# Zeroing the exponentials of later keys on GpSimd in two causal attentions

## The chip, the cores and the metric

The kernel runs on one core of a Trainium2 chip. The time is the device time of one execution in microseconds (us); for the kernel before, three runs are shown and their median is taken. One further execution was taken by the hardware profiler, and all durations of single instructions come from it. The engines are named as in the profile: PE is TensorE (its matmuls; PEld its weight loads), DVE is VectorE, ACT is ScalarE, POOL is GpSimd, and SP issues DMAs.

## The reference

The reference is a decoder of four layers, each with self-attention, cross-attention and a feed-forward part, on an input of 8 sequences of 256 tokens and 256 features. After each part comes `x = layernorm(x + part(x))`. Two of the self-attentions, those of layers 1 and 2, are causal with 16 heads of 16 features:

```python
attn = jnp.einsum('bqhd,bkhd->bhqk', q, k) * scale
causal = jnp.tril(jnp.ones((T, T), dtype=bool))
attn = jnp.where(causal, attn, -jnp.inf)
attn = jax.nn.softmax(attn, axis=-1)
out = jnp.einsum('bhqk,bkhd->bqhd', attn, v).reshape(B, T, C)
return out @ Wo + bo
```

(This is layer 2. Layer 1 has rotary positions on q and k and no bias.) Everything else of the reference is untouched by the change.

## The kernel before

The parts of the network run one after the other; the weights of the next part are loaded while one runs. The tokens are kept as `X` (tokens on partitions) and transposed as `xT` (features on partitions).

The two causal attentions are `l1_attn` (line 760) and `l2_attn` (line 730). Both hand a projection to `attention16` (line 593), which goes through the 8 sequences, called batches here. Queries and keys of two batches are projected at once (`pair`, line 600): batches 0 and 1 ahead of everything, batches 2 and 3 after batch 0, and so on, so batches 1, 3 and 5 have a projection right in front of them, and batches 2, 4 and 6 have none.

The softmax of a batch is made in two passes over the scores. First, `largest16` (line 451) computes scores with queries on partitions, and DVE takes the largest of each row. There are three steps: `short(0)` for the first 128 queries, and `long(0)` and `long(1)` for the last 128 queries and all 256 keys, each for half of the heads. `lower16` (line 491) transposes the negated maxima on PE and puts them into spare rows of the queries. Second, `exps16` (line 503) computes the scores again with keys on partitions; the maximum is now subtracted by the matmul itself, and ACT takes the exponentials straight from PSUM to SBUF. Here, too, there are three steps: `first(0)` and `first(1)` for the first 128 keys and all 256 queries (tile `e0`, one for each half of the heads), and `second` for the last 128 keys and the last 128 queries of all heads (tile `e1`). In both passes later keys are kept out by a mask: a matmul of the identity with a 128x128 tile that holds -1e30 above or below the diagonal is put into the PSUM bank first, and the scores are added to it (`four_banks`, line 432, which works on four banks of PSUM, four heads' groups at a time). `sums16` (line 555) multiplies the exponentials with the values; `divided16` (line 535) turns and divides the result, its last multiplication (line 553, tile `aT`) on POOL.

The steps of different batches are interleaved by hand in `attention16`: while batch b is exponentiated, the maxima of batch b+1 are taken (`ahead`), and the output projection of batch b-1 with its layer norm runs after the first of the three exponential steps (`before[0]`), its transposition at the end (`before[1]`). In the layer norm, DVE computes the statistics, POOL the reciprocal root (`rs_v` line 141 and `rs_y` line 143), and DVE then writes the normalised `X` in two instructions (line 187). The instructions of one engine run in the order in which they stand in its queue. The scores, the sums and the projections share 8 PSUM banks in turn (`bank`, line 408), so a set of four scores can start only once what stood in its banks has been read.

What the kernel prints below are the functions that the change touches and their callers.

Of the kernel before, what the change touches and what calls it, by code (L numbers as in the profile page):

```python
# [12 lines left out]
BF16 = mybir.dt.bfloat16  # L13
# [3 lines left out]
ALU = mybir.AluOpType  # L17
# [3 lines left out]
P = 128  # L21
# [21 lines left out]
class Net:  # L43
    def __init__(self, ctx: ExitStack, tc: tile.TileContext, ins, out):
        self.tc, self.nc, self.ins, self.out = tc, tc.nc, ins, out
        nc = self.nc
        self.const = ctx.enter_context(tc.tile_pool(name="const", bufs=1))
        self.wpool = ctx.enter_context(tc.tile_pool(name="weights", bufs=1))
        self.tmp = ctx.enter_context(tc.tile_pool(name="tmp", bufs=3))
        self.ps_t = ctx.enter_context(tc.tile_pool(name="ps_t", bufs=2, space=PSUM))  # L50

        self.ident = self.const.tile([P, P], F32, name="ident")
        make_identity(nc, self.ident)
        self.ones = self.const.tile([1, P], F32, name="ones")
        nc.gpsimd.memset(self.ones, 1.0)

        self.X = self.const.tile([P, NT, D], F32, name="X")
        self.xT = self.const.tile([P, 2, NTOK], F32, name="xT")
        self.xT4 = self.xT.rearrange("p c (t n) -> p c t n", n=P)
        for b in range(B):  # L60
            nc.sync.dma_start(
                self.X[:, 2 * b : 2 * b + 2, :],
                ins["x"][b].rearrange("(t p) d -> p t d", p=P),
            )
        self.cols = self.const.tile([P, ins["cols"].shape[1]], F32, name="cols")
        nc.scalar.dma_start(self.cols, ins["cols"])
        self.consts = self.const.tile([P, ins["consts"].shape[1]], F32, name="consts")
        nc.scalar.dma_start(self.consts, ins["consts"])
        self.earlier = self.const.tile([P, P], BF16, name="earlier")
        nc.vector.tensor_copy(self.earlier, self.cst("earlier"))  # L70
        self.causal = self.const.tile([P, P], BF16, name="causal")
        nc.vector.tensor_scalar(self.causal, self.cst("later"), -1e30, None, ALU.mult)

        self.later_k = self.const.tile([P, P], BF16, name="later_k")
        nc.vector.tensor_scalar(self.later_k, self.cst("sooner"), -1e30, None, ALU.mult)
        self.other = self.const.tile([P, P], BF16, name="other")
        nc.vector.tensor_scalar(self.other, self.cst("other"), -1e30, None, ALU.mult)
        self.ident_bf = self.const.tile([P, P], BF16, name="ident_bf")
        nc.vector.tensor_copy(self.ident_bf, self.ident)
        self.ones_bf = self.const.tile([P, P], BF16, name="ones_bf")  # L80
        nc.gpsimd.memset(self.ones_bf, 1.0)
        self.ctxT = self.const.tile([P, 2, NCTX], F32, name="ctxT")
        nc.scalar.dma_start(self.ctxT, ins["ctxT"].rearrange("p (c n) -> p c n", c=2))
        self.gate1 = self.const.tile([P, 2, 32], F32, name="gate1")
        nc.scalar.dma_start(self.gate1, ins["l1f_gate"].rearrange("p (c n) -> p c n", c=2))
        self.avg = self.const.tile([P, 2, B], F32, name="avg")
        self.w_scale = self.const.tile([P, len(L2X)], F32, name="w_scale")
        self.half = self.const.tile([P, 2], F32, name="half")
        nc.gpsimd.memset(self.half, -0.5)
        self.power = False  # L90
        dram = ctx.enter_context(tc.tile_pool(name="dram", bufs=1, space=bass.MemoryType.DRAM))

        self.xd1 = dram.tile([NTOK + 1, D], F32, name="xd1")
        self.one = self.const.tile([P, 1], F32, name="one")
        nc.gpsimd.memset(self.one, 1.0)
        self.wset = 0
# [406 lines left out]
    def exps16(self, qv, kv, sizes, causal, work):  # L503

        nc = self.nc
        rows = [slice(32 * r, 32 * r + 32) for r in range(4)]
        later = self.later_k.unsqueeze(1)
        n0 = sizes[0]
        e0 = [work.tile([P, 4, 2, 2 * P], F32, name="e0") for m in range(2)]
        e1 = work.tile([P, 4, 4, P], F32, name="e1", bufs=1) if causal else None  # L510

        def first(m):
            self.four_banks(
                [n0, 2, 2 * P],
                (lambda sc: sc[:, :, :P], later.to_broadcast([P, 2, P])) if causal else None,
                lambda r: [(u, kv[rows[r], u, m, :n0], qv[rows[r], u, m, :]) for u in range(2)],
                lambda r, sc: nc.scalar.activation(e0[m][:n0, r], sc, AF.Exp),  # L517
            )

        def second():  # L520
            self.four_banks(
                [P, 4, P],
                (lambda sc: sc, later.to_broadcast([P, 4, P])),
                lambda r: [
                    (2 * m + u, kv[rows[r], u, m, P:], qv[rows[r], u, m, P:]) for m in range(2) for u in range(2)
                ],
                lambda r, sc: nc.scalar.activation(e1[:, r], sc, AF.Exp),
            )

        def e(m, r, u, kb):  # L530
            return e1[:, r, 2 * m + u, :] if kb else e0[m][:n0, r, u, :]

        return [lambda: first(0), lambda: first(1)] + ([second] if causal else []), e

    def divided16(self, out, av, work, parts=1):

# [1362 lines left out]
def layouts(inp):  # L1899
# [74 lines left out]
    for n in "qkvo":  # L1974
# [6 lines left out]
    p = np.arange(P, dtype=np.float32)  # L1981
# [14 lines left out]
            ("cos", rope_cos),  # L1996
            ("sin", rope_sin),
            ("other", (p[:, None] % 16 != p[None] % 16).astype(np.float32)),
            ("sooner", (p[:, None] > p[None]).astype(np.float32)),
            ("earlier", (p[:, None] < p[None]).astype(np.float32)),  # L2000
        ],
        LAYOUT.consts,
# [45 lines left out]
```

## Time and profile before

| what | value |
|---|---|
| median of 3 runs | 2792.79 us (2783.5 to 2794.55) |
| the profiled execution | 2775.67 us |
| its span, first to last instruction | 2773.9 us |
| mean granted PE clock over the span | 0.873 |
| PE, DVE, ACT, POOL busy, share of the span | 78%, 61%, 35%, 32% |
| l1_attn, about 563 to 761 us: PE, POOL busy | 183.0 and 35.5 of 198 us |
| l2_attn, about 1290 to 1446 us: PE, POOL busy | 140.1 and 24.2 of 156 us |
| mask matmuls of `later_k` (line 440) | 192, of 256 or 512 columns |

Busy time adds up what an engine spends inside instructions; a wait for another engine is not in it. The profiler models the ends of matmuls, so how long a row of matmuls takes is better read from the start of one group to the start of the next. In the timeline, a line gives the start, the length, the engine, the source line and operation, the tile written and the tiles read, and in brackets how long the engine stood idle before it and what released it. Several instructions of one kind that follow one another are merged into one line (x4).

### The profile page before, as it was taken

Reading aid. Unit: us, or ns where it says so; the run is one execution under the profiler, and the core shown is the slowest. Engines: PE = TensorE matmul, PEld = TensorE weight load, DVE = VectorE, ACT = ScalarE, POOL = GpSimd, SP = SyncE. Lnnn points to the kernel's source line nnn. Section 1 sums busy time; section 2 is a strip of 40 time slices with the busy share of each in tenths; the row PEclk is TensorE's granted clock in tenths of the full one; section 3 lists DMA queues with packets and bytes.
Section 4 is the critical chain, followed back from the end, with each engine's and each line's share of the span. In section 5 each row is a group of like instructions: output and inputs, shape, how many; then the busy total and the mean of one; then the engine's idle time right before and its main releaser. Section 6 shows DMA issues by size and latency. Waiting matters only on the chain.

```text
span 2773.9 us, 40937 instructions
## 1 busy us (share of the span) xinstructions
PE 2171.2 (78%) x14331; PEld 1571.3 (57%) x14331; DVE 1681.6 (61%) x5714; ACT 957.4 (35%) x2197; POOL 891.8 (32%) x949
## 2 busy tenths in 40 slices
PE   8978688699988788438975767887878868777975
PEld 5554588555565467415544345666756656555654
DVE  4654300266667575356767876758668666654876
ACT  2322133234333442104432333343534435433431
POOL 1020121221111124451110136666566565660000
PEclk9988699899998779759997878889989888887987
DMA  2001243200010137420010011111111111120000
GB/s 81 2 1 42 105 149 108 69 7 1 1 62 16 36 106 220 141 80 1 1 42 16 1 65 46 45 43 47 38 41 47 40 43 43 52 73 3 1 20 12
DMA packets 84173, 135.04 MB, mean 49 GB/s; under 512 B 33445, under 2 KB 53045, under 8 KB 82048
## 3 DMA queue, kind: packets, MB, share of 16 engines
q0 software_dynamic: 52288, 79.27, 9.7%
q1 hardware_dynamic: 28924, 49.45, 5.3%
q10 hardware_dynamic: 2756, 3.72, 0.4%
q8 instruction: 114, 1.87, 0.3%
q14 instruction: 91, 0.75, 0.1%
HBM read 242.90 MB, written 17.70 MB: 94 GB/s over the span
## 4 chain that ended last, share of the span: by engine, by line
PE 25%; DVE 16%; issue 6%; ACT 3%; another core or an unknown queue 2%; POOL 2%; DMA 0%; ACTq 0%; POOLq 0%; DVEq 0%
PE po L1401 5%; PE pp L132 4%; PE s L132 4%; PE po L132 3%; DVE junk L1349 2%; DVE low L478 1%; PE ph L132 1%; PE s L1547 1%; PE sc L132 1%; PE s L1525 1%; POOL rows L893 1%; PE po L1382 1%; PE sc L445 1%; DVE X L187 1%
## 5 line engine op out<-in xcount | busy, mean ns | idle before, releaser
L893 POOL DMA_INDIRECT rows<-in_l2f_table_dram,index x512 | 530.5, 1036 | 348.8 <-issue 110.7
L1401 PE MATMUL po<-rows,diag 128*128 128x256 f32 x768 | 231.2, 437 | 90.7 <-ACT diag L1400 54.4
L1349 DVE SCALAR_TENSOR_TENSOR junk<-rows,X 128x256 f32<-128x256 f32 x512 | 214.9, 420 | 53.6 <-DMA rows<-in_l2f_table_dram,index 28.4
L1401 PEld LDWEIGHTS po<-rows,diag 128*128 128x128 f32 x768 | 153.0, 213 | 142.8 <-ACT diag L1400 67.2
L132 PE MATMUL pp<-xT,w 128*128 128x256 f32 (+1 forms) x672 | 196.9, 435 | 35.1 <-issue 20.4
L132 PE MATMUL ph<-xeT,we 128*128 128x128 f32 x1248 | 183.7, 291 | 20.9 <-DMA we<-in_l0f_experts_dram,wrow 16.5
L132 PEld LDWEIGHTS ph<-xeT,we 128*128 128x128 f32 x1248 | 170.1, 201 | 41.7 <-DMA we<-in_l0f_experts_dram,wrow 17.9
L553 POOL TENSOR_TENSOR aT<-sides,inv 128x256 f32<-128x256 f32 x64 | 46.8, 731 | 441.6 <-DVE sides L551 275.3
L132 PEld LDWEIGHTS pp<-xT,w 128*128 128x128 f32 x672 | 141.6, 218 | 69.2 <-issue 29.7
L1400 ACT ACTIVATE diag<-ident,dots 128x128 f32<-128x128 f32 x384 | 134.1, 394 | 129.9 <-PE po L1401 58.8
L173 PE MATMUL pt<-ident,X 128*128 128x128 f32 x352 | 76.3, 330 | 117.6 <-DVE X L187 68.9
L174 ACT COPY xT<-pt 128x512 f32<-128x512 f32 x88 | 51.6, 587 | 328.1 <-PE pt L173 229.7
L893 POOL DMA_INDIRECT xe<-xd,take x87 | 85.2, 979 | 208.0 <-PE pt L908 81.6
L141 POOL TENSOR_SCALAR rs_v<-ln_mv 128x2 f32<-128x2 f32 x48 | 12.5, 260 | 389.8 <-DVE ln_mv L164 362.1
L173 PEld LDWEIGHTS pt<-ident,X 128*128 128x128 f32 x352 | 49.4, 163 | 152.7 <-issue 73.0
L132 PE MATMUL py<-we,hT 128*128 128x256 f32 x496 | 129.8, 386 | 0.9 <-DVE hT L1037 0.9
L1014 DVE TENSOR_TENSOR y<-py,we 128x256 f32<-128x256 f32 x23 | 9.8, 425 | 199.0 <-PE py L132 199.0
L517 ACT ACTIVATE e<-sc 128x512 f32<-128x512 f32 (+1 forms) x155 | 82.0, 602 | 107.2 <-PE sc L445 93.5
L1008 ACT ACTIVATE hT<-ph,we 128x128 f32<-128x128 f32 x184 | 65.5, 367 | 121.0 <-PE ph L132 91.3
L187 DVE TENSOR_SCALAR X<-z,ln_mv,rs_y 128x256 f32<-128x256 f32 x192 | 73.3, 424 | 54.3 <-POOL rs_y L143 52.4
L445 PE MATMUL sc<-kv,qv 32*128 32x128 f32 (+2 forms) x1448 | 99.8, 315 | 2.5 <-DVE sides L551 1.0
L445 PE MATMUL sc<-qv,kv 32*128 32x128 f32 (+2 forms) x1396 | 99.1, 347 | 0.0
(492 smaller groups left out, 5205.2 us busy)
## 6 DMA issues: line engine op xcount, KB each, us to landing
we<-in_l1f_experts_dram SPq DMA_DIRECT2D x32, 384.0 KB
yd<-y SPq DMA_DIRECT2D x32, 256.0 KB
rows<-in_l2f_table_dram,index POOLq DMA_INDIRECT x512
w<-in_l2x_w_dram SPq DMA_DIRECT2D x1, 4096.0 KB
yd<-y SPq DMA_DIRECT2D x23, 128.0 KB
X<-in_x_dram SPq DMA_DIRECT2D x8, 256.0 KB
xd<-X ACTq DMA_DIRECT2D x8, 256.0 KB
xd<-X SPq DMA_DIRECT2D x8, 256.0 KB
```

The source lines that it names most:

```text
L132: self.nc.tensor.matmul(out, lhsT=lhsT, rhs=rhs, start=n == 0, stop=n == last and bias is None)
L173: nc.tensor.transpose(pt[:, c, j, :], self.X[:, i0 + j * step, c * P : (c + 1) * P], self.ident)
L174: nc.scalar.copy(self.xT4[:, :, i0 : i0 + step + 1 : step, :], pt)
L187: nc.vector.tensor_scalar(self.X[:, i, :], z[:, j, :], mv[:, j, 0:1], r[:, j : j + 1], ALU.subtract, ALU.mult)
L445: nc.tensor.matmul(sc[: shape[0], part], lhsT=lhsT, rhs=rhs, start=mask is None, stop=True, skip_group_check=True)
L517: lambda r, sc: nc.scalar.activation(e0[m][:n0, r], sc, AF.Exp),
L553: nc.gpsimd.tensor_tensor(out, split(both), split(inv), ALU.mult)
L893: self.nc.gpsimd.indirect_dma_start(out=out, out_offset=None, in_=table, in_offset=bass.IndirectOffsetOnAxis(ap=index, axis=0), **({} if r ...
L1008: nc.scalar.activation(hT[:, g + f, :], ph[:, f, :], AF.Gelu, bias=b1[:, g + f : g + f + 1])
L1349: nc.vector.scalar_tensor_tensor(junk, row, 1.0, self.X[:, i, :], ALU.mult, ALU.mult, accum_out=out)
L1400: nc.scalar.activation(diag, self.ident, AF.Copy, scale=dots[:, k : k + 1])
L1401: nc.tensor.matmul(po, lhsT=diag, rhs=rows[:, k, D:], start=False, stop=g + k == H * K - 2)
```

## The change

The mask `later_k` goes out: the tile, the constant it was made from, and the mask matmuls in the three exponential steps. The scores of later keys are therefore exponentiated as they are. After each step, one affine selection on POOL goes over the exponentials of that step in place and writes 0 where the key (partition) comes after the query (last index). The selection of `first` covers the first 128 queries of each head, [128, 4, 2, 128] elements, with gaps between the rows of 128; that of `second` covers all of `e1`, [128, 4, 4, 128]. The maxima keep their own mask (`causal`). Last, the step `second` is put ahead of `first(0)` and `first(1)`.

```diff
-        self.later_k = self.const.tile([P, P], BF16, name="later_k")
-        nc.vector.tensor_scalar(self.later_k, self.cst("sooner"), -1e30, None, ALU.mult)
...
-        later = self.later_k.unsqueeze(1)
         n0 = sizes[0]
+
+        def no_later(e):
+
+            nc.gpsimd.affine_select(
+                out=e, in_=e, compare_op=ALU.is_ge, fill=0.0, base=0,
+                pattern=[[0, n] for n in e.shape[1:-1]] + [[1, P]], channel_multiplier=-1,
+            )
         e0 = [work.tile([P, 4, 2, 2 * P], F32, name="e0") for m in range(2)]
         e1 = work.tile([P, 4, 4, P], F32, name="e1", bufs=1) if causal else None
 
         def first(m):
             self.four_banks(
                 [n0, 2, 2 * P],
-                (lambda sc: sc[:, :, :P], later.to_broadcast([P, 2, P])) if causal else None,
+                None,
                 lambda r: [(u, kv[rows[r], u, m, :n0], qv[rows[r], u, m, :]) for u in range(2)],
                 lambda r, sc: nc.scalar.activation(e0[m][:n0, r], sc, AF.Exp),
             )
+            if causal:
+                no_later(e0[m][:, :, :, :P])
 
         def second():
             self.four_banks(
                 [P, 4, P],
-                (lambda sc: sc, later.to_broadcast([P, 4, P])),
+                None,
...
                 lambda r, sc: nc.scalar.activation(e1[:, r], sc, AF.Exp),
             )
+            no_later(e1)
...
-        return [lambda: first(0), lambda: first(1)] + ([second] if causal else []), e
+        return ([second] if causal else []) + [lambda: first(0), lambda: first(1)], e
...
-            ("sooner", (p[:, None] > p[None]).astype(np.float32)),
```

## The prediction

> **What bounds the kernel now.** I read the page's first two parts first, to see whether one engine is the limit. TensorE (PE) is busy 78% of the span, VectorE (DVE) 61%, GpSimd (POOL) 32%. In the two stretches that the change touches PE is nearly full and POOL nearly empty.
>
> ```profile
> PE 2171.2 (78%) x14331; PEld 1571.3 (57%) x14331; DVE 1681.6 (61%) x5714; ACT 957.4 (35%) x2197; POOL 891.8 (32%) x949
> ...
> 563.00:761.00 198.00, 183.04 (x1750) 111.12 (x1749) 130.96 (x275) 74.98 (x133) 35.49 (x42) 0.99 0.01 1
> 1290.00:1446.00 156.00, 140.07 (x1608) 87.28 (x1607) 106.26 (x238) 68.79 (x122) 24.16 (x34) 1.00 0.01 2
> ```
>
> The last two lines are the windows view of l1_attn and l2_attn: length, then busy time of PE, weight load, DVE, ACT, POOL, then granted PE clock. PE at 92% and 90% says that removing PE work pays in full. A busy share is no chain, though, so I followed one batch in the timeline (641 to 660 us, l1_attn, batch 2, which has no projection in front of it).
>
> ```profile
> 644.09 0.38 PE L440 MATMUL sc<-causal,ident_bf 128*128 128x512 bf16 x1 [0.45 <-DVE sides L551]
> 649.76 0.22 POOL L141 TENSOR_SCALAR rs_v<-ln_mv 128x2 f32<-128x2 f32 x1 [4.92 <-DVE ln_mv L164]
> 650.07 0.71 POOL L143 TENSOR_TENSOR rs_y<-rs_v,half 128x2 f32<-128x2 f32 x1
> 650.81 0.73 DVE L187 TENSOR_SCALAR X<-z,ln_mv,rs_y 128x256 f32<-128x256 f32 x2 [1.13 <-POOL rs_y L143]
> 651.46 2.48 DVE L478 TENSOR_REDUCE low<-sc 128x2 f32<-128x512 f32 x4
> 653.39 0.27 PE L440 MATMUL sc<-causal,ident_bf 128*128 128x256 bf16 x1 [0.33 <-DVE low L478]
> 653.99 0.27 PE L440 MATMUL sc<-causal,ident_bf 128*128 128x256 bf16 x1 [0.33 <-DVE low L478]
> 657.90 0.33 PE L497 MATMUL sc<-ident,low 128*128 128x128 f32 x1 [0.88 <-DVE low L478]
> ```
>
> Columns: start, length, engine, work, and the idle time before it with its releaser. PE waits four times per batch, each time for DVE to free a PSUM bank or finish a maximum. The loop that sets the batch's length is: sums end, DVE turns and merges `sides`, the fourth mask of the short maxima gets its bank, short scores, four reductions, z and its statistics, POOL's `rs_y`, DVE's two normalisations X, four reductions (first long), four banks free, second long scores, four reductions, last transpose, rest of the sums. The masks taken away are not in it.
>
> [...] in l0_attn:
>
> ```profile
> 174.88 0.73 DVE L187 TENSOR_SCALAR X<-z,ln_mv,rs_y 128x256 f32<-128x256 f32 x2 [1.65 <-POOL rs_y L143]
> 176.16 0.71 POOL L143 TENSOR_TENSOR rs_y<-rs_v,half 128x2 f32<-128x2 f32 x1
> 176.84 1.26 POOL L284 TENSOR_TENSOR biased<-X,bo 128x512 f32<-128x512 f32 x1
> 176.91 1.66 DVE L187 TENSOR_SCALAR X<-z,ln_mv,rs_y 128x256 f32<-128x256 f32 x2 [0.50 <-POOL rs_y L143]
> ```
>
> The same pair of X takes 0.73 us with POOL idle, and 1.66 us when a POOL instruction of 1.26 us stands right behind `rs_y` and starts 0.07 us before it: 0.93 us lost. [...]
>
> ```profile
> 584.10:587.50 3.40, 2.07 (x13) 1.05 (x12) 3.22 (x6) 0.00 (x0) 0.00 (x0) 1.00 0.00 0
> 587.50:590.90 3.40, 3.40 (x28) 2.41 (x26) 1.41 (x2) 0.00 (x0) 0.00 (x0) 0.50 0.02 7
> ```
>
> Over the whole trace's clock record, of 56 full-clock windows with PE busy under 45%, 53 were followed by half clock; of those at 45 to 70%, 10 of 64.
>
> **Part 1, masks removed.** Four masks of 256 columns take 0.54 us from start to start (622.37 to 622.90 at later_k), four of 512 columns 0.97 us (631.11 to 632.08). A batch has two sets of the first and one of the second: 2.05 us, times 16 batches 32.8 us. That is the gain if PE set the end throughout. By the loop above:
> - Batches 2, 4, 6 of each attention: the first exponentials' mask is followed by the wait for `sides` (fixed by DVE at 644.04), the other two by waits for long reductions that start only after X. Gain 0; the time becomes PE idle.
> - Batches 1, 3, 5 follow the projection of a pair, so PE's own front sets the first short scores: the first mask, 0.54, counts. 6 x 0.54 = 3.2 us.
> - Batch 0 has no output projection and no X: PE feeds the long scores undelayed, so 0.54 + 0.97 = 1.5 us, twice 3.0 us.
> - Batch 7 has no maxima ahead; its end is the last exponentials, and a selection now follows them, about 1.2 us, against 1.5 us of masks: 0, give or take 1 us each.
> Sum: -6 us. The DVE instruction at the start and 64 KB of constants hide under the loads.
>
> **Part 2, selections added.** Per batch one of 2048 elements per partition and two of 1024; 48 in all. The one affine selection in this trace has 128 elements:
>
> ```profile
> masks.py:199 POOL TENSOR_SCALAR_AFFINE_SELECT ident<-ident x1: 285/285/285, 1.4 to 1.4; 128x128 f32<-128x128 f32 x1
> ```
>
> Per element: not under 0.83 ns, what memsets show ((1.37 - 0.52) us over 1024 elements); not over 1.95, if the 250 ns to the next POOL start were all elements. [...] I take 1.0 ns and 0.16 us fixed: 1.18 us and 2.2 us (bounds 1.03 to 2.0, and 1.9 to 4.0). As work this is hidden: 4.6 us per batch on an engine with some 80% of each batch free. The sums of half m=0 need selections that ended long before; half m=1 begins over 4 us after its exponentials. Queued behind the large selection are `rs_v` and `rs_y`: its exponentials end at 645.35, it ends near 647.7, `rs_v` is due at 649.7. Cover 2.0 us; at 4.0 us per selection it is gone.
>
> **Part 3, what the small selection meets.** POOL's order after the change is large selection, `rs_v`, `rs_y`, small, small, aT, aT. The first small one waits for exponentials that end at 651.15 now, and at 650.6 without their mask, just before `rs_y` ends (650.78). So it stands ready behind `rs_y` [...] 0.05 us before X asks, as `biased` did. X loses 0.93 - (1.26 - 1.18) = 0.85 us, and X is on the loop. If X won, its second instruction would be held instead. Batches 1 to 6, twice: 12 x 0.85 = +10 us (bounds 8 to 20, the latter with a 2.0 us selection).
>
> **Part 4, the clock.** PE now reaches the second long masks earlier and their banks come later: after its third exponential scores (done near 651.2) it has four masks until about 654.9. With 0.27 us busy each, that is 2.6 us idle in 3.7. Set against free-running windows, about half or a little more of the positions put one window under 45%. I take 7 of 12 batches, each with 3.4 us at half clock, 1.7 us lost in scores and sums that are on the loop: +12 us (bounds 0 to 25).
>
> **The second exponentials put first** add nothing: they give the large selection the time above. One-buffered `e1` is free by then, since its readers stand ahead on PE.
>
> **Sum.** -6 + 10 + 12 = +16 us on the profiled execution's 2775.67 us (span 2773.9 and 1.8 around it), so 2792. The median of the runs, 2792.79, lies 17 us above that execution; the difference carries over: 2809.
>
> **Rivals.**
> *PE is the bound after all* (other side): DVE's waits shift along with PE, the loop shrinks by every mask, and the selection arrives after X. For it: PE 92% busy. Against it: four waits per batch that name DVE. 2793 - 33 = 2760. It decides if the maxima's banks stop being waited for. Chance 0.12.
> *No hold*: the selection comes over 0.8 us after `rs_y` and X is through. Only part 1 is left: 2787. The margin of 0.2 us in part 3 speaks for and against. 0.11.
> *Hold, but the clock stays*: idle splits over windows. 2793 - 6 + 10 = 2797. 0.16.
> *Slow selection*: at 1.6 ns or more, 1.8 us, the first X is held 1.5 us and the next small selection, ready 2.1 us after the first, holds the second X by up to as much again; the large one reaches `rs_v`. 12 x 3 = 36, less 6, and clock 12: about 2835, up to 2855. Two strided dimensions, not in the trace, speak for it; 285 ns speaks against. 0.19.
>
> **Numbers.** My forecast, with its own range 2799 to 2822, has 0.42. What a measurement here tells from no change is 0.5%, 14 us: 2779 to 2807. About 0.4 of the forecast lies inside. Faster 0.12 + 0.01; same 0.10 + 0.15 + 0.17 = 0.42; slower 0.25 + 0.19 + 0.01 = 0.45. The range 2786 to 2840 leaves out the PE-bound case and the far part of the slow selection.
>
> **What would show it.** Right: X pairs of 1.4 to 1.7 us in both causal attentions, a selection overlapping each; longer waits for `low` at the second long masks; half-clock stretches between 600 and 760 us. Wrong: X pairs at 0.73, or batches without projection (19.3 us now) under 18 us. A small selection well over 1.2 us would void the sizes, not the mechanism.

## The result and the profile after

The kernel with the change takes 2822.71 us (median of 4 runs, 2814.42 to 2835.24), beside 2789.76 us for the kernel before (4 runs). The ratio is 1.0121, 95% interval 1.0078 to 1.0163: slower, by about 34 us by the ratio and 33 by the medians. The profiled execution took 2814.42 us, its span 2812.7, which is 38.8 more than the span of before.

The page after, with the parts on engines and on groups of instructions. In the last line, behind the bars: busy time and mean ns of one, then idle time of the engine ahead of them.

```profile
PE 2183.4 (78%) x14130; PEld 1579.1 (56%) x14139; DVE 1691.6 (60%) x5713; ACT 957.3 (34%) x2197; POOL 961.0 (34%) x997
...
L184 DVE TENSOR_SCALAR X<-z,ln_mv,rs_y 128x256 f32<-128x256 f32 x192 | 82.7, 473 | 55.5 <-POOL rs_y L140 52.9
```

PE has about 200 matmuls fewer (192 masks) and is busy for 12 us *longer*; POOL has 48 instructions and 69 us more. The mean X has grown from the 424 ns of before to 473. The windows view of after, over both causal attentions and over one stretch inside the first (length, then busy time of PE, weight load, DVE, ACT, POOL, then granted PE clock):

```profile
596.00:798.00 202.00, 181.61 (x1696) 111.97 (x1694) 127.47 (x251) 71.72 (x133) 62.77 (x62) 0.90 0.00 1
1324.00:1482.00 158.00, 135.12 (x1436) 84.92 (x1434) 105.69 (x225) 63.88 (x115) 52.43 (x54) 0.89 0.01 1
660.50:667.30 6.80, 6.28 (x37) 3.45 (x36) 3.70 (x7) 0.69 (x2) 1.10 (x1) 0.50 0.00 0
```

The clock, 0.99 and 1.00 before, is 0.90 and 0.89. The third line is one of nineteen stretches at half clock in the two attentions (0.50 in the column of the clock). The timeline of after shows what surrounds it, in batch 2 of l1_attn (start, length, engine, line and work, idle time before it with its releaser):

```profile
656.73 0.22 POOL L138 TENSOR_SCALAR rs_v<-ln_mv 128x2 f32<-128x2 f32 x1 [2.33 <-DVE ln_mv L161]
657.03 0.71 POOL L140 TENSOR_TENSOR rs_y<-rs_v,half 128x2 f32<-128x2 f32 x1
657.75 1.10 POOL L508 TENSOR_SCALAR_AFFINE_SELECT e<-e 128x1024 f32<-128x1024 f32 x1
657.77 1.54 DVE L184 TENSOR_SCALAR X<-z,ln_mv,rs_y 128x256 f32<-128x256 f32 x2 [1.14 <-POOL rs_y L140]
659.24 2.47 DVE L475 TENSOR_REDUCE low<-sc 128x2 f32<-128x512 f32 x4
659.97 0.27 PE L437 MATMUL sc<-causal,ident_bf 128*128 128x256 bf16 x1 [1.11 <-DVE low L475]
660.57 0.37 PE L437 MATMUL sc<-causal,ident_bf 128*128 128x256 bf16 x1 [0.33 <-DVE low L475]
661.16 0.37 PE L437 MATMUL sc<-causal,ident_bf 128*128 128x256 bf16 x1 [0.23 <-DVE low L475]
...
662.07 2.09 PE L442 MATMUL sc<-kv,qv 32*128 32x256 f32 x16
```

The small selection starts 0.02 us before X, and the X pair takes 1.54 us; before it took 0.73. The reductions behind it start later, and PE, which has no masks of the exponentials left to do, waits for them before the next mask of the maxima, 1.11 us for the first bank alone. 16 long scores then take 2.09 us at half clock, where the equal set of `long(0)`, at 656.01 and at full clock, took 1.15 us.

Summed over the time between 575 and 1480 us, the waits view of after has these two lines for the second long masks, which wait for banks that DVE has yet to read (the banks go by two names, `sc` and `pt`; the numbers are the total, the number of waits and the longest, in us):

```profile
PE sc L437 <- DVE low L475: 20.6, 38, 1.5
PE pt L437 <- DVE low L475: 8.4, 17, 1.4
```

and the same view of before these:

```profile
PE sc L440 <- DVE low L478: 7.3, 23, 0.3
PE pt L440 <- DVE low L478: 1.9, 6, 0.3
```

The view of the selection's line in after gives its durations (least, median, greatest, in ns) and who waited for it:

```profile
L508 POOL TENSOR_SCALAR_AFFINE_SELECT e<-e x48: 1101/1102/2035, 596.6 to 1477.9; 128x1024 f32<-128x1024 f32 x32, 128x2048 f32<-128x2048 f32 x16
...
  PEld sc L572: 2.4, 5
  PE sc L572: 1.3, 3
```

The zeros are thus late for hardly anything: 3.7 us at most, nearly all in the two last batches.

To compare kernels I measured three things in each trace. The *stage time* is the length of l1_attn from its first rotary addition on POOL to its last `rs_y`, plus that of l2_attn from the first GELU of its keys to its last `rs_y`: 220.9 + 197.1 = 418.0 us before, 240.2 + 214.5 = 454.7 after, +36.7. The *half clock* is how much of that the trace's clock record shows at 0.5: 3.4 us before, 101.9 after. The *X pair* is the time of the two X instructions of a batch. Stage times come from one execution each and scatter by a few us (e4 below, for which nothing was to be expected, differs by 3.0), and what lies outside the stages scatters too, from 2347 to 2366 us in the kernels e1 to e8; so a ratio and a stage time can lie up to 9 us apart (e2).

### The profile page after: what moved, and what is told of

It is laid out like the page before. It is cut to its first block, busy times and chain, and to the rows that moved or that the text cites. A ratio compares the mean times of both kernels' runs of the same rounds, so it can differ in the third digit from the quotient of the medians.

```text
span 2812.7 us, 40594 instructions
## 1 busy us (share of the span) xinstructions
PE 2183.4 (78%) x14130; PEld 1579.1 (56%) x14139; DVE 1691.6 (60%) x5713; ACT 957.3 (34%) x2197; POOL 961.0 (34%) x997
## 4 chain that ended last, share of the span: by engine, by line
PE 25%; DVE 14%; issue 6%; another core or an unknown queue 3%; POOL 3%; ACT 3%; DMA 1%; POOLq 0%; ACTq 0%; DVEq 0%
PE po L1407 5%; PE pp L129 4%; PE s L129 4%; PE po L129 3%; POOL rows L899 2%; PE sc L129 1%; PE ph L129 1%; DVE junk L1355 1%; PE s L1553 1%; PE s L1531 1%; DVE low L475 1%; PE po L1388 1%; DVE X L184 1%; DMA rows<-in_l2f_table_dram,index 1%
## 5 line engine op out<-in xcount | busy, mean ns | idle before, releaser
L1355 DVE SCALAR_TENSOR_TENSOR junk<-rows,X 128x256 f32<-128x256 f32 x512 | 215.0, 420 | 42.6 <-DMA rows<-in_l2f_table_dram,index 19.6
L170 PE MATMUL pt<-ident,X 128*128 128x128 f32 x352 | 85.4, 361 | 123.8 <-DVE X L184 79.1
L170 PEld LDWEIGHTS pt<-ident,X 128*128 128x128 f32 x352 | 55.1, 179 | 161.9 <-issue 78.4
L184 DVE TENSOR_SCALAR X<-z,ln_mv,rs_y 128x256 f32<-128x256 f32 x192 | 82.7, 473 | 55.5 <-POOL rs_y L140 52.9
L442 PE MATMUL sc<-qv,kv 32*128 32x128 f32 (+2 forms) x1392 | 106.9, 349 | 0.0
```

What stands on the lines that cost most here:

```text
L170: nc.tensor.transpose(pt[:, c, j, :], self.X[:, i0 + j * step, c * P : (c + 1) * P], self.ident)
L184: nc.vector.tensor_scalar(self.X[:, i, :], z[:, j, :], mv[:, j, 0:1], r[:, j : j + 1], ALU.subtract, ALU.mult)
L442: nc.tensor.matmul(sc[: shape[0], part], lhsT=lhsT, rhs=rhs, start=mask is None, stop=True, skip_group_check=True)
L1355: nc.vector.scalar_tensor_tensor(junk, row, 1.0, self.X[:, i, :], ALU.mult, ALU.mult, accum_out=out)
```

## The experiments

The theory is that of the prediction: two losses, the hold of X behind the small selection, and a PE clock that falls when PE idles where the masks were. The rivals: the loss is the selections as such (late zeros, POOL's queue); or the new order of the steps; or the clock alone, with the hold unimportant.

| kernel | ratio to its kernel before | 95% interval | stage time against 418.0 | half clock, us | X pair, us |
|---|---|---|---|---|---|
| the change | 1.0121 | 1.0078 to 1.0163 | +36.7 | 101.9 | 1.49 to 1.54 |
| e1, one small selection | 1.0082 | 1.0050 to 1.0114 | +15.9 | 47.2 | 0.73 |
| e2, masks kept | 1.0036 | 1.0019 to 1.0052 | +19.4 | 33.9 | 1.5 to 1.65 in 8 of 12 |
| e3, no selection | 1.0036 | 1.0020 to 1.0053 | +11.7 | 59.6 | 0.73 |
| e4, order alone | 0.9990 | 0.9973 to 1.0008 | +3.0 | 10.9 | 0.73 |
| e5, the change, X on POOL | 0.9977 | 0.9956 to 0.9998 | -3.1 | 38.1 | 2.43 (POOL) |
| e6, before, X on POOL | 0.9980 | 0.9946 to 1.0014 | -5.6 | 9.5 | 2.43 (POOL) |
| e7, the change, scores twice | 1.0082 | 1.0052 to 1.0111 | +22.7 | 50.5 | 1.49 to 1.54 |
| e8, e3 with scores twice | 1.0010 | 0.9991 to 1.0029 | +0.3 | 16.1 | 0.73 |
| e9, before, X late | 1.0126 | 1.0103 to 1.0149 | +33.4 | 40.9 | off the loop |
| e10, the change, X late | 1.0113 | 1.0089 to 1.0137 | +34.1 | 64.4 | off the loop |
| e11, e10 with scores twice | 1.0123 | 1.0096 to 1.0150 | +28.8 | 46.2 | off the loop |
| e12, e9, turned later | 0.9961 | 0.9946 to 0.9975 | -8.9 | 4.7 | off the loop |

Each ratio is taken against runs of the kernel before on the same chip. Beside e9 to e12 these took 2650 to 2651 us, not 2776; the difference lies behind the two stages (from the last `rs_y` of l2_attn to the last instruction it is 1324.8 us in the profile of before and 1204.2 in that of e12), so their times are read by ratio and stage alone.

### Undoing the parts

**e1** merges the two small selections into one of 2048 elements behind `first(1)`:

```diff
-        e0 = [work.tile([P, 4, 2, 2 * P], F32, name="e0") for m in range(2)]
+        if causal:
+            e01 = work.tile([P, 2, 4, 2, 2 * P], F32, name="e0", bufs=1)
+            e0 = [e01[:, m] for m in range(2)]
+        else:
+            e0 = [work.tile([P, 4, 2, 2 * P], F32, name="e0") for m in range(2)]
...
-            if causal:
-                no_later(e0[m][:, :, :, :P])
+            if causal and m:
+                no_later(e01.rearrange("p m r u q -> p (m r u) q")[:, :, :P])
```

> One selection of 2048 elements for both halves of e0, after the last exponential, in place of two of 1024; all else as in the changed kernel, which is 33 us above the kernel before. Theory (hold and clock): nothing stands behind rs_y any more, so the pair of X is back from 1.54 to 0.73 us; 12 batches x 0.8 = 10 us less, and PE idles 0.8 us less per batch, so that part of the half clock goes as well: 8 to 18 us above before. Rival 1, the sums wait for the selections: this one ends a microsecond later, so 40 us above before or more. Rival 2, the clock falls by the missing masks alone and the hold is beside the point: about 31 us above before, with X at 0.73.

The ratio is 1.0082, some 23 us above the kernel before, beyond the expected 8 to 18; the stage time is up by 15.9. By ratio alone e1 can't be told from the change, whose interval overlaps; the stage times and the clock record tell them apart. The groups of e1 show that X is free:

```profile
L184 DVE TENSOR_SCALAR X<-z,ln_mv,rs_y 128x256 f32<-128x256 f32 x192 | 71.9, 417 | 53.8 <-POOL rs_y L140 52.9
...
L508 POOL TENSOR_SCALAR_AFFINE_SELECT e<-e 128x2048 f32<-128x2048 f32 x32 | 64.3, 2009 | 124.8 <-ACT e L536 77.1 <-ACT e L524 47.7
```

With the same number of selected elements and no hold, 20.8 us of the 36.7 of stage time are gone; the half clock has fallen with it, from 101.9 to 47.2. So the hold matters, and more than by its own length: it also lengthens the idle time of PE, whose waits for `low` at the second long masks add up to 29.0 us in the change and 20.2 in e1. At the other end the last batch pays, where one large selection now stands behind the last exponentials: the last interval from `rs_y` to `rs_y` is 17.5 us in both stages, where the kernel before has 13.5 and 12.9. That is 8.5 of the 15.9 us; each of the two has 6.8 us of half clock in it, so not all of it is the selection.

**e2** keeps the change and puts the mask matmuls back into the three exponential steps:

```diff
-                None,
+                (lambda sc: sc[:, :, :P], later.to_broadcast([P, 2, P])) if causal else None,
...
-                None,
+                (lambda sc: sc, later.to_broadcast([P, 4, P])),
```

> The changed kernel with the masks put back ahead of the exponentials, so that the selections write zeros over zeros: PE has its old work, POOL its new one. Theory (hold and clock): the hold stays, X pairs at 1.54 us, 12 x 0.8 = 10 us; the idle time of PE is filled by masks again, so half clock in the two attentions falls from 99 us to under 40: 10 to 16 us above before. Rival 1, selections late for the sums: as the changed kernel or worse, 33 to 40 us above. Rival 2, the masks' removal lowers the clock whatever X does: 10 us above, with no half clock left at all.

The ratio is 1.0036, some 10 us, as expected; the half clock is 33.9 us. The stage time is up by more, 19.4, while what lies outside the stages was 8.6 us shorter in that execution than in that of before. X is held in 8 of 12 batches. In the other four it is not, and the timeline of e2 shows why; the first three lines are batch 2 of l1_attn, the others batch 4:

```profile
655.50 0.71 POOL L142 TENSOR_TENSOR rs_y<-rs_v,half 128x2 f32<-128x2 f32 x1
656.25 1.65 DVE L186 TENSOR_SCALAR X<-z,ln_mv,rs_y 128x256 f32<-128x256 f32 x2 [1.14 <-POOL rs_y L142]
656.66 1.10 POOL L511 TENSOR_SCALAR_AFFINE_SELECT e<-e 128x1024 f32<-128x1024 f32 x1 [0.44 <-ACT e L523]
...
713.90 0.71 POOL L142 TENSOR_TENSOR rs_y<-rs_v,half 128x2 f32<-128x2 f32 x1
714.65 0.73 DVE L186 TENSOR_SCALAR X<-z,ln_mv,rs_y 128x256 f32<-128x256 f32 x2 [1.14 <-POOL rs_y L142]
715.06 1.28 POOL L511 TENSOR_SCALAR_AFFINE_SELECT e<-e 128x1024 f32<-128x1024 f32 x1 [0.45 <-ACT e L523]
```

In both the selection comes 0.41 us after X has started, that is, between its two instructions. Once the selection wins and the second X is held (1.65 us); once X wins and the selection is longer by 0.18 us (1.28). With the masks the selections come later, and the outcome hangs on some hundredths of a us: in l1_attn the selection won when it came 0.383 and 0.405 us after the start of X, and lost at 0.410 to 0.412. Without them, in the change, the selection always stood ready first.

**e3** is the change without any selection; the later keys stay in the sums.

```diff
-                no_later(e0[m][:, :, :, :P])
+                pass
...
-            no_later(e1)
```

> The changed kernel without the three selections: no mask and no zeroing, so later keys are left in the sums. What is left is the removal of the masks and the new order. Theory (hold and clock): X pairs at 0.73 us, -6 us by the masks that are in the loop, some half clock (20 to 50 us of it, 5 to 12 us lost): 0 to 8 us above before. Rival, PE is the bound and the selections cost it all: 33 us below before. Rival 2, the clock falls by the missing masks alone: 20 to 25 us above before.

No gain at all: 1.0036, some 10 us *slower* than the kernel before, a little outside the range, with 59.6 us of half clock. So PE's missing masks cost time although nothing was put in their place, and POOL has no part in that.

**e4** is the kernel before with the second exponentials put first.

```diff
-        return [lambda: first(0), lambda: first(1)] + ([second] if causal else []), e
+        return ([second] if causal else []) + [lambda: first(0), lambda: first(1)], e
```

> The kernel before with second put ahead of first(0) and first(1), masks and all. Theory: the order alone moves no more than 3 us either way, with no new half clock. Rival, the order itself starves PE or the maxima: 8 us or more above before.

0.9990, interval 0.9973 to 1.0008. The order is out.

### The hold and the clock by themselves

**e5** and **e6** give X to POOL in the two causal attentions, in the change and in the kernel before, so that no X on DVE meets a selection there:

```diff
-            nc.vector.tensor_scalar(
+            (nc.gpsimd if self.causal_part else nc.vector).tensor_scalar(
...
+            net.causal_part = name in ("l1_attn", "l2_attn")
```

> The changed kernel with the two normalisations X of the causal attentions on POOL, right behind rs_y and ahead of the small selections, in place of DVE. [...] DVE no longer waits 1.1 us for rs_y nor spends 0.7 us on X. Theory (hold and clock; DVE's loop sets a batch): up to 1.8 us less per batch against the kernel before, in 12 batches, less what half clock is left: 0 to 25 us below before. Rival, the selections are late for the sums: still 20 us or more above before, since POOL has only got more to do.

> The kernel before (masks, no selections) with the same two normalisations on POOL. Theory (DVE's loop sets a batch, with rs_y and X in it): PE stands idle some 2 us of each batch of 19.3 us, so a batch gets 1 to 1.8 us shorter: 12 to 22 us below before, and the clock stays, PE being fuller than it was. Rival, PE sets the batch: X on POOL changes nothing, within 4 us of before.

e5 is 0.9977 (0.9956 to 0.9998), about 6 us below the kernel before; the stage time is 40 us below that of the change. e6, by its interval between 15 us below and 4 above, and 5.6 below by stage time, was expected 12 to 22 below: that estimate was too high. Batches without projection fell from 19.3 to 19.6 us to 18.5 to 18.7 in e6 and to 18.0 to 18.3 in e5. None of these intervals has half clock in it, and each of e5's is 0.4 to 0.7 us shorter than e6's: with X out of DVE's queue the missing masks seem to count where in the loop of before they were worth nothing (no run has them alone with X on POOL). The group of X in e5 tells its price on POOL:

```profile
L184 POOL TENSOR_SCALAR X<-z,ln_mv,rs_y 128x256 f32<-128x256 f32 x32 | 39.0, 1227 | 1.7
```

1.23 us each, 2.43 us per batch. DVE no longer stands in wait for `rs_y` there (between 575 and 1480 us X on DVE waits for it 24 times before, 30.0 us in all, and 8 times in e5, 10.5 us) and has no X to do, which is what the batches gain; the last intervals, 17.0 and 17.2 us in e5 where the change has 14.5 and 13.9, give some of it back.

**e7** lets PE compute the scores of `first(1)` twice, in the change, and **e8** does it without selections (later keys stay in the sums). The second time writes the same scores again; it puts PE work ahead of the second long scores, where PE idles in the change.

```diff
-        for parts in zip(*(heads(r) for r in range(4))):
+        for parts in [p for _ in range(times) for p in zip(*(heads(r) for r in range(4)))]:
...
+                times=2 if causal and m else 1,
```

> The changed kernel with the scores of first(1) computed twice into the same banks (1.08 us more of PE per batch, the same values). PE does more, in the place where it idles before the second long maxima. Theory (hold and clock): the hold stays (X pairs 1.5 us) but half clock falls from 102 us to under 60: faster than the changed kernel by 8 to 20 us, though PE has more to do; 12 to 25 us above before. Rival, half clock comes from elsewhere, or is not what costs: as the changed kernel or up to 13 us slower.

> As the run without selections (no mask, no zeroing, so later keys stay in the sums), with the scores of first(1) computed twice. That run was 10 us above before with 60 us of half clock. Theory (clock): with the idle time filled, half clock is under 20 us, and what is left is what the masks were worth in the loop: 0 to 6 us below before, though PE computes 128 sets of scores more. Rival, half clock is not what costs: 10 us or more above before.

The added work makes both kernels *faster*, by stage time; by ratio the interval of e7 overlaps with that of the change, and e8's with e3's. The windows view over the two stages, first of e3, then of e8:

```profile
573.70:800.30 226.60, 204.84 (x1943) 128.91 (x1942) 142.13 (x292) 85.02 (x153) 40.70 (x51) 0.94 0.01 4
1254.60:1457.70 203.10, 174.48 (x1840) 111.90 (x1840) 134.12 (x295) 82.75 (x145) 28.27 (x39) 0.92 0.01 2
```

```profile
570.60:792.40 221.80, 201.78 (x2071) 129.94 (x2070) 142.11 (x292) 85.05 (x153) 40.81 (x51) 0.98 0.01 4
1250.50:1447.00 196.50, 169.41 (x1968) 109.90 (x1968) 134.08 (x295) 82.73 (x144) 28.38 (x40) 0.98 0.01 3
```

There are 128 matmuls more per stage, and yet PE is busy for 3 to 5 us less, with the clock at 0.98 where e3 has 0.94 and 0.92. DVE, ACT and POOL do the same in both. Half clock falls from 59.6 to 16.1 us and the stage time by 11.4: 0.26 us lost per us of half clock. From the change to e7 it falls from 101.9 to 50.5 and the stage time by 14.0: 0.27. e7 keeps the hold and remains 1.0082; e8, without it, is level with the kernel before, where 0 to 6 us below was expected. e7 minus e8 is 22.4 us of stage time: 9.4 of hold, 34.4 us of half clock, which is 9.3 at 0.27, and 3.7 more, of which 2.7 lie in the last intervals.

The single intervals from one `rs_y` to the next (the last ones left out) show the same more sharply. Four of twelve have no half clock in either e3 or e8, and there the two kernels agree to 0.01 us: the added matmuls cost nothing. In the other eight e3 alone has half clock, 40.5 us of it, and is 10.3 us longer in sum: 0.25 us per us, between 0.17 and 0.30 in single intervals. Six have none in either e7 or e8; there e7 is longer by 0.75 to 0.81 us, which is what its X pair is longer by: the hold goes into the batch in full.

### A version that beats both

In the kernel before, DVE stands still for 1.1 us per batch waiting for `rs_y`, with the long reductions queued behind X: in batch 2 of l1_attn their scores end at about 650.6, X waits until 650.81, and the first of them starts at 651.46. **e9** moves X (and its transposition on PE) behind the next batch's sums; a small DVE instruction makes it depend on that division. **e10** does this in the change, **e11** adds the scores twice.

```diff
+            if late:
+                z, mv, r = kept[0]
+                r2 = work.tile([P, 2], F32, name="r2")
+                nc.vector.scalar_tensor_tensor(r2, self.last_div, 0.0, r, ALU.mult, ALU.add)
+                for j in range(2):
+                    nc.vector.tensor_scalar(
+                        self.X[:, 2 * b + j, :], z[:, j, :], mv[:, j, 0:1], r2[:, j : j + 1], ALU.subtract, ALU.mult
+                    )
             self.transpose_into_xT(2 * b, 1)
```

> The kernel before with the normalised X of a causal batch moved behind the sums of the next batch: X then waits for the division of that next batch by a dependency made for it (one small VectorE instruction more per batch), so the reductions no longer stand behind the wait for rs_y. My theory (VectorE's chain with that wait is the loop): batches of the causal attentions are 1 to 1.8 us shorter in 12 of 16, no half clock above 15 us in the two stages together, the total 8 to 22 us below the kernel before. Rival (the wait is replaced by another one of the same length, as when X went to GpSimd): within 5 us.

> The changed kernel with X moved in the same way. My theory: the small selection no longer meets X behind rs_y, so pairs of X take 0.73 us or cost nothing where they lie; the masks' time and the wait for rs_y are gained, some half clock remains (20 to 60 us in the two stages). The total is 15 below to 10 above the kernel before, so 30 to 50 below the changed kernel. Rival (most of the changed kernel's loss is the clock whatever X does): over 80 us of half clock, 10 to 30 above the kernel before.

> The same with the scores of the second small exponential step computed twice, so that TensorE has work where the masks were. If the half clock is what is left over in the run before this one, it falls below 20 us and the total is 10 to 25 below the kernel before, and below the run with X moved alone. If TensorE's own work is the bound once X is out of the way, the total rises by up to 20 us over that run.

All three missed: 1.0126, 1.0113 and 1.0123, each some 30 us slower. The timeline of e9, batch 2 of l1_attn, shows the new wait:

```profile
642.83 0.50 PE L445 MATMUL sc<-kv,qv 32*128 32x128 f32 x6
...
643.11 0.41 DVE L598 TENSOR_SCALAR X<-z,ln_mv,r 128x256 f32<-128x256 f32 x1
...
643.58 0.33 PE L173 MATMUL pt<-ident,X 128*128 128x128 f32 x1 [0.25 <-DVE X L598]
...
647.72 1.48 PE L445 MATMUL sc<-kv,qv 32*128 32x128 f32 x12
...
648.83 2.48 DVE L462 TENSOR_REDUCE low<-sc 128x4 f32<-128x512 f32 x4 [4.59 <-PE sc L445]
```

The transposition now stands in PE's queue among the first and the short scores and waits for X. Once it is through, PE works off what it holds up, partly at half clock (0.74 granted from 643.5 to 649.1), and the short scores end at 649.2; DVE's short reductions idle 4.59 us for them, 1.55 before. DVE's wait had gone and PE's had come. With that wait in the loop, these three kernels can't tell what clock or masks are worth without a hold.

**e12** leaves X where e9 has it and transposes it a batch later:

```diff
-            if before and not causal:
-                before[1]()
+            if older or (before and not causal):
+                (older or before)[-1]()
```

> The kernel before with X moved behind the next batch's sums as in the run before, but with its transposition on TensorE a batch later, so that TensorE no longer waits for X ahead of the short scores. If that wait was what made the batches without projection 1.6 us longer, they fall from 21.0 us to 18.3 to 18.7 us (long reductions start when their scores are there, 0.8 us earlier than in the kernel before), and the total is 4 to 12 below the kernel before. If the small instruction and X on VectorE behind the division are what costs, they stay above 19.4 us and the total is not below the kernel before.

0.9961, 0.9946 to 0.9975: about 10 us below the kernel before, inside what was expected. So the place of the transposition was what e9 had lost by, its wait and the half clock that came with it (40.9 us, 4.7 in e12) taken together. Batches without projection take 18.3 to 18.7 us, 19.3 to 19.6 before, though DVE has one instruction more in each. The timeline of e12 shows batch 4 of l1_attn with X in its new place:

```profile
696.43 0.15 DVE L595 SCALAR_TENSOR_TENSOR r<-div,rs_y 128x2 f32<-128x2 f32 x1
...
696.62 1.17 DVE L597 TENSOR_SCALAR X<-z,ln_mv,r 128x256 f32<-128x256 f32 x2
698.06 1.29 DVE L462 TENSOR_REDUCE low<-sc 128x4 f32<-128x512 f32 x2 [0.27 <-PE pt L445]
...
702.54 0.71 POOL L143 TENSOR_TENSOR rs_y<-rs_v,half 128x2 f32<-128x2 f32 x1
703.12 0.69 DVE L478 TENSOR_REDUCE low<-sc 128x2 f32<-128x512 f32 x1 [0.97 <-PE sc L445]
```

X sits in a gap that DVE had anyway, and is done 0.27 us before the short scores are. The long reductions start at 703.12, before `rs_y` has ended. Even here X is held for a while: 1.17 us, beside `aT` of 0.72 us on POOL, where the pair alone takes 0.73; in the gap that costs nothing.

## Why the prediction was right, step by step

It said slower by 16 us, 2809 in a range of 2786 to 2840; it is 2822.71, slower by 33, twice as much, and just above the forecast's own narrower range of 2799 to 2822. Direction and the two causes were right, the size of the clock's part was not. That the result still lies within the wide range is in part luck: two errors in Part 4 pull in opposite directions. The sum came out as follows, in us over both stages:

| step | predicted | measured | from |
|---|---|---|---|
| masks, batches 2, 4, 6 | 0 | 0.00 to 0.01 per batch | e8 against before, `rs_y` to `rs_y`; e3 where it has no half clock |
| masks, batches 1, 3, 5 | -3.2 | -2.3 | e8: -0.31 to -0.42 in the four such intervals; six times 0.39 |
| batch 0 | -3.0 | no gain seen | start to first `rs_y`: +2.9 and +3.6, of which half clock there makes some 4.5 in all |
| last batches | 0, give or take 1 each | +0.1 | 14.51 and 13.89 after, 13.53 and 12.94 before, less 0.9 each for the 3.4 us of half clock in them |
| hold of X | +10 | +9.4 | sums of the twelve X pairs: 18.2 and 8.8 |
| clock | +12 | +26.6 | 98.5 us more of half clock at 0.27 |
| sum | +16 | +36.7 | stage times; 2.9 are not assigned, most of it ahead of the first `rs_y` |

**Part 1** held in its main point: in a chain with four waits on DVE, PE's masks are worth nothing where a wait for DVE follows, though PE was busy 92% of the time. The gain in batch 0 did not come. The rival *PE is the bound after all* would have made e3 33 us faster; it was 10 slower.

**Part 2**: 1.10 us and 2.02 us for the selections, 1.18 and 2.2 predicted, so (2.02 - 1.10) us over 1024 elements or 0.90 ns per element; the 1.0 ns of the prediction was its author's estimate, between bounds of 0.83 and 1.95. At 0.90 ns some 0.2 us of each selection are left as fixed. The strided form costs nothing more (in e1 2.00 to 2.01 us for 2048 elements in rows with gaps, 2.01 to 2.03 without), and the rival *slow selection* falls. Its cover was there: sums waited 3.7 us for zeros at most.

**Part 3** was right to the place and nearly to the size: the selection starts 0.02 to 0.08 us before X (0.05 predicted) in all twelve batches, and costs 0.78 us per pair (0.85 predicted). The size was an estimate from one pair of X in l0_attn, which lost 0.93 us beside a POOL instruction of 1.26 us. By what means POOL holds X was not shown; what the runs show is that the pair takes 0.73 us alone and 1.49 to 1.54 when a selection of 1.10 us has started just ahead of it. The rival *no hold* had only the 0.2 us of margin on its side.

**Part 4** is the step that was mis-sized, in both of its factors. The count: it took seven stretches of one window of 3.4 us, 24 us in all, each behind a window with PE busy under 45%. (In the clock records of before and after every stretch but the last, which the end cuts off, is a whole multiple of 3.41 us long: these are the windows. The 45% come from the prediction's count in the trace of before, where half clock followed 53 of 56.) The stages of the change have 98.5 us more of half clock than those of before, in nineteen stretches, eleven of them 6.8 us or longer. Three windows of the clock record of after, around the second long masks of batch 2 in l1_attn, show how that comes about (columns as in the windows view above):

```profile
657.08:660.49 3.41, 2.04 (x21) 1.25 (x16) 2.71 (x5) 2.55 (x6) 1.76 (x2) 1.00 0.00 0
660.49:663.91 3.42, 2.89 (x19) 1.42 (x18) 1.22 (x3) 0.11 (x1) 1.10 (x1) 0.50 0.00 0
663.91:667.32 3.41, 3.41 (x22) 2.05 (x18) 2.49 (x4) 0.59 (x1) 0.00 (x0) 0.50 0.00 0
```

In the first PE is busy 60%, and half clock follows; in the second, at half clock, 85%, and it goes on; in the third 100%, and it ends. I counted the same for every window of the two stages of after. Half clock followed each of the sixteen full-clock windows with PE busy under 60%, two of the seven at 60 to 70%, and none of the 80 above. It went on after eleven of the twelve half-clock windows with PE busy under 95%, and after none of the eighteen above. So the place was right, but all twelve batches fell there, not seven: four behind a window under 45%, six at 45 to 60%, two at 60 to 70%. With the windows by which they went on, these are 72 us. The other 30 us lie ahead of the first `rs_y` and in the last batches.

The prediction also gave the clock nothing without a hold: of the rival *no hold* it said that only part 1 is left. The missing masks alone make 56 us of half clock (e3), the hold alone, with masks kept and in 8 of 12 batches, 30 (e2), and both together 98.5. Both lengthen the same idle time of PE: its waits for `low` at the second long masks, `sc` and `pt` together, are 9.2 us before, 19.2 in e3, 17.1 in e2, 29.0 in the change.

The loss per us: the prediction took half of a stretch as lost, 0.5, as if PE set the end throughout. It is 0.25 to 0.27. The likely reason is that during much of a stretch PE waits for DVE, whose four reductions take 2.47 us in a stretch at half clock and took 2.48 at full. With 98.5 us and the predicted 0.5 the result would have been some 23 us slower still. The rival *hold but the clock stays* is refuted by the clock record.

**The order** cost nothing, as said.

What stays open: PE's busy share sorts the windows of the change well, but not those of all kernels. Over the stages of all fourteen traces, half clock followed 32 of the 65 full-clock windows with PE busy 45 to 60%; what decides there, these runs don't show. e10 and e11, in which PE waits elsewhere, still have 64 and 46 us of half clock, and e7, with PE work just ahead of the second long scores, 50.5. Why batch 0 gained nothing is not known either. Another order of the selections in the last batch was not tried.

## What to carry to other kernels

Before taking work from a busy engine, follow one turn of its loop and see which wait ends behind that work: a 92% busy PE gained 0.4 us in some batches and none in others. Where PE then idles, price the clock too (a us at half clock cost 0.25 to 0.27 us here), count every way in which its idle time grows, work taken away and banks freed later alike, and look for stretches longer than one window of 3.41 us (eleven of nineteen here). When an instruction moves to POOL, look for DVE instructions that POOL can hold, as it held X here (1.49 to 1.54 us for 0.73) and not the four reductions (2.47 us beside the second small selection, 2.48 before), and that become ready within its length, behind an instruction of POOL's above all; and when a wait is moved, move what is queued behind it as well, or it turns up on the next engine (e9 against e12).

## What the runs showed of the hardware

- More PE work made a stage faster: 128 matmuls more per stage cut PE's own busy time by 3 to 5 us and the two stages together by 11.4 us, with the clock at 0.98 in place of 0.94 and 0.92 (e8 against e3).
- In the stages of the change half clock followed every full-clock window of 3.4 us with PE busy under 60% (16 of 16) and none busy over 70% (0 of 80); it ended after a half-clock window with PE busy over 95% (18 of 18), and after one busy less only once in twelve.
- A us at half clock cost 0.26 and 0.27 us in a loop that alternates between PE and DVE, in two pairs of runs, and 0.25 over the eight intervals that can be compared one by one.
- A selection that starts between two X instructions wins or loses by hundredths of a us: it takes 1.10 us and the pair of X 1.65, or it takes 1.28 and the pair 0.73 (e2).
- The normalising instruction of 128x256 takes 1.23 us on POOL and 0.41 on DVE, and yet the changed kernel was faster with it on POOL, 0.9977 against 1.0121 of the kernel before (e5): the hold of 0.78 us per pair was gone, and so were DVE's waits of some 1.1 us for `rs_y`.
